# Edge sums by half tiles: one-hots side by side on PE, target rows spread on chip

## The chip, the cores and the metric

One core of one Trainium2 chip runs the whole model: a graph layer, a linear attention and a mixture of experts over 3125 nodes and 50,000 edges, in fp32. The metric is the device time of one execution in microseconds (us). The engines are named as in the profile: PE (TensorE, matrix products; PEld is its loading of stationary operands), DVE (VectorE), ACT (ScalarE), POOL (GpSimd, which also issues indirect DMAs) and SP (SyncE, which issues DMAs).

## The reference

Rows of 512 features are a scalar part of 128 and a vector part of 128x3. The change is in the edge part of the graph layer. Cut to what matters, with `x` the layer-normed rows:

```python
pd0, ip1 = p0[edge_dst], einsum('eum,eum->eu', p1[edge_dst], p1[edge_src]) / 3
w = ssp(edge_attr @ W_f1) @ W_f2 * (ssp(concat(pd0, pd0, ip1) @ W_s1) @ W_s2)
w1, w2, w3, w4 = split(w, 4)
x0e, x1e = split_irreps(x[edge_src])
out0 = w1 * x0e * sh0 + w4 * (einsum('eum,em->eu', x1e, sh1) / sqrt(3))
out1 = w2 * x0e * sh1 + w3 * x1e * sh0
out = segment_sum(concat(out0, out1), edge_dst, num_segments=3125)
```

`p0`, `p1` are linear maps of the rows, `ssp` is softplus less log 2, and `sh0`, `sh1` (one and three numbers) belong to the edge. Before it come layer norm, the node maps and a linear attention; after it an output map, a second layer norm, and eight experts of which each row takes two.

## The kernel before, in words

Three stages follow each other.

Stage 1 makes two tables in DRAM, `rows_d` (what an edge needs of its target: 32 hidden features and 384 of `p1`) and `rows_s` (what it needs of its source: 384 of `p1` and the 512 mapped features). Beside that it makes a record of 48 numbers for each edge (`records`, lines from 255: four `sh` numbers, both indices, the place of the target within its group in column 6, and 32 features of `ssp(edge_attr @ W_f1)`), and sorts the records by target. Targets are cut into 25 groups of 125. DVE counts the edges of each group (line 201), and `places(c)` (lines 229 to 252) finds the slot of each edge in chunk `c` of 14: a comparison with all groups, a running sum (line 239), a product and a reduction. POOL then writes 128 records at a time to their slots in `recs` (line 417, 391 times), between the node work. `recs` is cleared first (line 166). Each group's records begin at a new pair.

Stage 2 works through `recs`. Four tiles of 128 edges are a quad, two are a pair; 204 pairs are run. The order on PE, ACT, DVE and POOL is written out by hand in `run_pairs`, so that in step `s` different pairs are at different points: `fetch` (pair s+9) loads records and has POOL gather target rows `gd` (line 730) and source rows `gx` (line 734), one row per edge each; `products` (L746, DVE) multiplies the two `p1` parts; `turn` (L754, PE) sums and transposes the products, ACT copies them (L763); `hidden` (L770 to 780, PE) makes the hidden features of four tiles side by side in four column strips of the array; `softplus` (ACT) and `softplus2` (DVE) follow; `weigh` (L819, L823) makes the two factors of `w` on PE in four row strips, ACT copies one to SBUF and DVE multiplies by the other (L830). `dots` and `dots2` make the sum of vector features times `sh1` (L840 ACT, L848 and L850 DVE). `feats` (L878, L885, L889, L894) makes the features `ft`, with `sh1` applied by ACT. `which` (L860) makes a one-hot of the edge's target within the group, 128 wide, and `gather_up` (L902) multiplies one-hot by features, which sums the edges per target in PSUM. `keep_sums` (L911, DVE) adds a pair's sums to the group's rows of `acc`. Between pairs POOL issues copies of the expert weights into rows that can be gathered (`line_up`, L918, 32 of 1 MB).

Stage 3 maps the sums, writes `out`, normalizes, chooses experts, and runs 53 tiles of 128 rows through the experts' layers, with weights gathered by POOL.

Of the kernel before, what the change touches and what calls it, by code (L numbers as in the profile page):

```python
# [18 lines left out]
TG = 125  # L19
D = 512  # L20
# [11 lines left out]
NPR_MOST = 204  # L32
# [13 lines left out]
def gnn_mix_moe_kernel(ctx: ExitStack, tc: tile.TileContext, a: dict, out: bass.AP):  # L46
# [13 lines left out]
    NPR = (EDGES - NG) // (PR * P) + NG  # L60
    whole, rest_e = divmod(EDGES, P)
    TE = whole + (rest_e > 0)
    NQ = (NPR * PR + G - 1) // G
# [29 lines left out]
    pair_tile = const.tile([P, NPR], I32, name="pair_tile")  # L93


    rows_d = dram.tile([N, HID + 3 * MUL], F32, name="rows_d")
    rows_s = dram.tile([N, 3 * MUL + D], F32, name="rows_s")
    lined = dram.tile([T // CT, P, CT, REC], F32, name="lined")
    recs = dram.tile([NQ * G * P, REC], F32, name="recs")
# [20 lines left out]
    tok = counted(const, "tok", [[TG, NT]], [P, NT], channel=1)  # L120
# [8 lines left out]
    with ExitStack() as c1:  # L129
        srt = c1.enter_context(tc.tile_pool(name="srt", bufs=1))  # L130
        ints = c1.enter_context(tc.tile_pool(name="ints1", bufs=1))
        pair_no = counted(srt, "pair_no", [[1, NPR]], [P, NPR])
# [21 lines left out]
        for r in range(4):  # L154
# [6 lines left out]
        zw = NQ * G * REC // 10  # L161
        zero = tmp.tile([P, zw], F32, name="zero")
        nc.vector.memset(zero, 0.0)
        flat = recs.rearrange("s f -> (s f)")
        cleared = [
            nc.gpsimd.dma_start(
                flat[k * P * zw : (k + 1) * P * zw].rearrange("(p f) -> p f", p=P), zero
            )
            for k in range(10)
        ]  # L170

# [14 lines left out]
        in_tile_i = tmp.tile([P, T], I32, name="in_tile_i")  # L186
        nc.vector.tensor_scalar(in_tile_i, to_i, 4195.0, None, op0=ALU.mult)
        nc.vector.tensor_single_scalar(in_tile_i, in_tile_i, 19, op=ALU.arith_shift_right)
        in_tile = tmp.tile([P, T], F32, name="in_tile")
        nc.vector.tensor_copy(in_tile, in_tile_i)  # L190
        to_f = tmp.tile([P, T], F32, name="to_f")
        nc.vector.tensor_copy(to_f, to_i)
        local = tmp.tile([P, T], F32, name="local")
        nc.vector.scalar_tensor_tensor(local, in_tile, -float(TG), to_f, op0=ALU.mult, op1=ALU.add)

        NC = T // CT
        hot = tmp.tile([P, NT, CT + 1], F32, name="hot")
        sums = tmp.tile([P, NT], F32, name="sums")
        here = tmp.tile([P, T], F32, name="here")
        for b in range(NT):  # L200
            nc.vector.tensor_scalar(
                here, in_tile, float(b), 0.0, op0=ALU.is_equal, op1=ALU.add, accum_out=sums[:, b : b + 1]
            )
# [225 lines left out]
        for c in range(1, NC):  # L429
            records(c)  # L430
            for t in range((c - 1) * NT // (NC - 1), c * NT // (NC - 1)):
                place(8 * t + 42)
                place(8 * t + 50, layer_norm(t))
# [997 lines left out]
```

## Time and profile before

Times are of the device. The profiled execution is a separate one, slower than the runs without a profile.

| what | us |
|---|---|
| median of 3 runs (2772.86 to 2774.89) | 2774.01 |
| the profiled execution, own time | 2957.7 |
| its span, from the first to the last instruction | 2955.8 |
| stage 1: to the last node row (DMA of `rows_s`) | about 704 |
| stage 2: first gather to last sum | 721.9 to 2022.1 |
| first and last start of `gather_up`'s products | 774.4 and 2021.0 |
| PE busy in the span | 2533.0 (86%) |
| DVE busy | 1785.0 (60%) |
| ACT busy | 1393.6 (47%) |
| POOL busy | 1719.6 (58%) |
| mean granted clock of PE | 0.936 of full |

Three views of the profile are used. The windows view gives the busy time of each engine in a stretch of the span, with the number of instructions in brackets, then the clock granted to PE, the mean busy share of the 16 DMA engines, and what they moved. The timeline lists instructions in order of time: start, duration, engine, line of the kernel, operation, output and inputs by the program's names, shape, and how many were merged into the row; a bracket at the end tells idle time and what ended it. The view of groups gives, for all instructions of a line and shape, their busy time, the mean duration, and the idle time before them. A duration includes a fixed latency, so that the next instruction of an engine can start before it ends; the pitch, from start to start, is what an instruction costs in a full engine.

### The profile page before, as it was taken

What the parts mean: (1) busy time and instruction counts of PE and PEld (TensorE: products, weight loads), DVE (VectorE), ACT (ScalarE), POOL (GpSimd) and SP (SyncE); (2) the same over time, 40 slices, a digit from 0 to 9 for tenths busy, and PEclk for the clock granted to TensorE, in tenths of its full rate; (3) what the DMA queues carried; (4) which work ended last, traced back from release to release, by engine and by line L of the source; (5) the groups of instructions that cost most, each with busy time, mean ns of one, the idle gap of its engine ahead of it and who ended that gap; (6) DMA issues with size and microseconds to landing.
All of it is one profiled execution on the core that took longest, in us unless ns stands there. A gap on an engine that the chain in (4) does not pass through costs nothing. (4 is left out here: it accounts for less than half of the span.)

```text
span 2955.8 us, 44464 instructions
## 1 busy us (share of the span) xinstructions
PE 2533.0 (86%) x14742; PEld 1593.7 (54%) x14742; DVE 1785.0 (60%) x3666; ACT 1393.6 (47%) x3960; POOL 1719.6 (58%) x1723
## 2 busy tenths in 40 slices
PE   2466594885699999999999999997599999999997
PEld 2344242553344444444444444445488888888886
DVE  4755450223699999999999999998422222222221
ACT  1334241110588888877888888885211111111111
POOL 0766657664766666666666666641355555555552
PEclk9767796897799999999999999999799999999998
DMA  6435202554788888787888888855722623956361
GB/s 259 148 126 175 85 21 66 168 174 137 245 256 255 256 255 254 256 248 247 254 259 262 261 263 262 253 177 187 279 66 72 239 69 119 329 202 244 112 223 51
DMA packets 189190, 577.23 MB, mean 195 GB/s; under 512 B 54177, under 2 KB 78662, under 8 KB 176920
## 3 DMA queue, kind: packets, MB, share of 16 engines
q0 software_dynamic: 132912, 485.72, 51.1%
q1 hardware_dynamic: 49704, 82.29, 8.2%
q10 hardware_dynamic: 6336, 6.28, 0.7%
q8 instruction: 121, 1.98, 0.3%
q14 instruction: 117, 0.96, 0.1%
HBM read 624.55 MB, written 119.50 MB: 252 GB/s over the span
## 5 line engine op out<-in xcount | busy, mean ns | idle before, releaser
L902 PE MATMUL ps_s<-ft,one 128*128 128x512 f32 x1632 | 745.7, 600 | 19.4 <-issue 14.2
L730 POOL DMA_INDIRECT gd<-rows_d,rec x408 | 434.4, 1065 | 269.0 <-issue 87.2
L417 POOL DMA_INDIRECT recs<-again,at_i x391 | 400.8, 1025 | 231.6 <-issue 110.5
L902 PEld LDWEIGHTS ps_s<-ft,one 128*128 128x128 f32 x1632 | 294.1, 190 | 396.0 <-issue 318.7
L734 POOL DMA_INDIRECT gx<-rows_s,rec x408 | 400.9, 983 | 144.8 <-issue 102.4
L885 ACT ACTIVATE ft<-ft,rec 128x128 f32<-128x128 f32 x1224 | 380.2, 389 | 201.9 <-DVE ft L878 143.0
L1306 ACT ACTIVATE h<-ps_f,bias 128x128 f32<-128x128 f32 x318 | 110.7, 367 | 671.5 <-PE ps_f L1293 622.1
L1293 PE MATMUL ps_f<-h,we 128*128 128x128 f32 x3392 | 406.8, 278 | 16.7 <-ACT h L1306 15.1
L1293 PEld LDWEIGHTS ps_f<-h,we 128*128 128x128 f32 x3392 | 388.8, 192 | 30.7 <-ACT h L1306 25.0
L1308 DVE TENSOR_SCALAR h<-ps_f,bias 128x128 f32<-128x128 f32 x318 | 108.2, 350 | 481.6 <-PE ps_f L1293 456.9
L1220 POOL DMA_INDIRECT we<-w_rows,w_at x212 | 214.3, 1011 | 266.6 <-PE ps_y L1324 102.0
L830 DVE TENSOR_TENSOR wt<-wt,wb 128x1024 f32<-128x1024 f32 x204 | 247.6, 1214 | 29.9 <-PE ps_h L775 21.9
L840 ACT ACTIVATE dot<-gx,rec 128x128 f32<-128x128 f32 x816 | 261.4, 398 | 0.0
L819 PE MATMUL wa<-w_f,hT 32*128 32x512 f32 x816 | 240.2, 642 | 3.7 <-issue 2.6
L823 PE MATMUL wb<-w_s,hT 32*128 32x512 f32 x816 | 241.7, 644 | 0.0
L1293 PEld LDWEIGHTS ps_f<-xt,we 128*128 128x128 f32 x1696 | 200.1, 194 | 26.0 <-issue 24.9
L746 DVE TENSOR_TENSOR prod<-gd,gx 128x768 f32<-128x768 f32 x204 | 194.0, 951 | 31.0 <-DMA gx<-rows_s,rec 31.0
L1293 PE MATMUL ps_f<-xt,we 128*128 128x128 f32 x1696 | 200.5, 277 | 0.7 <-ACT xt L1241 0.7
L754 PEld LDWEIGHTS ps_ip<-ident,prod 128*128 128x128 f32 x1224 | 136.3, 144 | 118.7 <-issue 118.7
L889 DVE TENSOR_TENSOR ft<-gx,wt 128x768 f32<-128x768 f32 x204 | 197.6, 969 | 0.0
L1324 PE MATMUL ps_y<-we,h 128*128 128x512 f32 x424 | 196.1, 605 | 0.2
L754 PE MATMUL ps_ip<-ident,prod 128*128 128x128 f32 x1224 | 161.3, 283 | 40.7 <-issue 40.7
(306 smaller groups left out, 3599.2 us busy)
## 6 DMA issues: line engine op xcount, KB each, us to landing
w_rows<-in_Wh POOLq DMA_DIRECT2D x24, 1024.0 KB
rows_s<-r SPq DMA_DIRECT2D x24, 448.0 KB
recs<-zero POOLq DMA_DIRECT2D x10, 1056.0 KB
rec<-recs SPq DMA_DIRECT2D x102, 96.0 KB
lined<-rec SPq DMA_DIRECT2D x14, 672.0 KB
again<-lined POOLq DMA_DIRECT2D x14, 672.0 KB
w_rows<-in_Wo POOLq DMA_DIRECT2D x8, 1024.0 KB
gd<-rows_d,rec POOLq DMA_INDIRECT x408
```

The lines of the kernel that those rows point to most:

```text
L417: put = nc.gpsimd.indirect_dma_start(out=recs[:, :], out_offset=bass.IndirectOffsetOnAxis(ap=at_i[:m, t : t + 1], axis=0), in_=again[c][:m ...
L730: nc.gpsimd.indirect_dma_start(out=Q.gd[:, (i + 2) % G, :], out_offset=None, in_=rows_d[:, :], in_offset=bass.IndirectOffsetOnAxis(ap=reci ...
L734: Q.last = nc.gpsimd.indirect_dma_start(out=Q.gx[:, i, :], out_offset=None, in_=rows_s[:, :], in_offset=bass.IndirectOffsetOnAxis(ap=reci[ ...
L754: nc.tensor.matmul(ps[:, i, :], Q.prod[:, i, b * P : (b + 1) * P], ident, is_transpose=True, start=(b == 0), stop=(b == 2),)
L819: nc.tensor.matmul(wa[:, k, :], Q.hT[r, 0, :], w_f2[r, :], start=True, stop=True)
L823: nc.tensor.matmul(wb[:, k, :], Q.hT[r, 1, :], w_s2[r, :], start=True, stop=True)
L830: nc.vector.tensor_mul(R.wt, R.wt, wb)
L840: nc.scalar.activation(R.dot[:, c - 1, k, :], x[:, i, c * MUL : (c + 1) * MUL], AF.Copy, scale=Q.rec[:, i, c : c + 1])
L885: nc.scalar.activation(R.ft[:, k, D + c * MUL : D + (c + 1) * MUL], R.ft[:, k, 2 * D :], AF.Copy, scale=Q.rec[:, i, c : c + 1],)
L902: nc.tensor.matmul(R.ps, R.one[:, k, :], R.ft[:, k, m * D : (m + 1) * D], start=(k == 0 and m == 0), stop=(k == 1 and m == 1),)
L1220: nc.gpsimd.indirect_dma_start(out=dst, out_offset=None, in_=src, in_offset=bass.IndirectOffsetOnAxis(ap=at[:, j : j + 1], axis=0), bounds ...
L1293: nc.tensor.matmul(pss[f], ws[l][:, k, f * P : (f + 1) * P], h[:, k, :], start=(k == 0), stop=(k == 3))
```

## The change

Edges are sorted by 50 groups of targets, alternately 63 and 62, instead of 25 of 125. Two such groups make a half tile each; a pair now holds one tile of 128 edges from either half, and each half has room for 8 tiles (1024 edges) in a fixed place. Edges over that go to up to 12 overflow pairs behind the 200 fixed ones; for more there is a loop. Slots without an edge are no longer all cleared in DRAM: only the last quad of each group and the overflow pairs are, and records of slots without an edge are masked on chip (`clear`).

- The one-hot (`which`) is 64 wide and made per quad. ACT multiplies it by each of the four `sh` numbers (`scaled`), so `dots`, `dots2` and the `sh` steps of `weigh` and `feats` go. `feats` makes eight products of 128 features instead.
- `gather_up` puts the two halves in two column strips of 64 of the array, with four one-hots each: the first over 512 columns, the others over two runs of 128. All eight pairs of a group add up in one PSUM bank, which ACT copies to `acc` once (`kept`); only overflow pairs are still added by DVE.
- Target rows are no longer gathered per edge. `targets` loads the 64 rows of each half once per group on SP; `over` transposes the one-hots on PE, and `own_rows` multiplies them by the rows, in two row strips, which gives each edge its target's `p1` in PSUM. `products` reads it there; `hidden` takes the 32 hidden features by a product too.
- `weigh` alternates its two products, and ACT copies the first in one piece. `hidden2` copies the hidden features to SBUF before softplus.
- In stage 1, `places` counts over 50 groups and sends edges past 1024 to overflow slots; the expert weights are copied (`line_up`) from ACT's queue during stage 1.
- In the order written out, `keep_sums`, `softplus2` and `products` come first on DVE in a step, before `which`.
- `acc` holds 128 rows a tile, with two unused; stage 3 reads and writes each tile of `own` and `out` in two DMAs, and `xs` in one.

```diff
...
-NPR_MOST = 204
+NOV_MOST = 12
...
         cleared = [
-            nc.gpsimd.dma_start(
-                flat[k * P * zw : (k + 1) * P * zw].rearrange("(p f) -> p f", p=P), zero
-            )
-            for k in range(10)
+            nc.gpsimd.dma_start(by_quad[:, qs, :], zero[:, : G * REC].unsqueeze(1).to_broadcast([P, n, G * REC]))
+            for qs, n in (
+                (slice(per - 1, NFIX // PR, per), NG), (slice(NFIX // PR, (NFIX + NOV_MOST) // PR), NOV_MOST // PR),
+            )
         ]
...
-        for b in range(NT):
+        for b in range(NU):
...
+            nc.vector.tensor_copy(hot[:, :, 0], from_ if c == 0 else upto[:, :, CT])
...
+                hot[:, :, 1:], in_half[:, ts].unsqueeze(1).to_broadcast([P, NU, CT]),
+                lane[:, :NU].unsqueeze(2).to_broadcast([P, NU, CT]), op=ALU.is_equal,
...
+            nc.vector.tensor_mul(hot[:, :, 1:], upto[:, :, 1:], hot[:, :, 1:])
+            nc.vector.tensor_reduce(slot, hot[:, :, 1:].rearrange("p b i -> p i b"), AX.X, ALU.add)
             nc.vector.tensor_copy(slot_i, slot)
-            at = at_i[:, c * CT : (c + 1) * CT]
+            nc.vector.tensor_single_scalar(rank, slot_i, 65535, op=ALU.bitwise_and)
+            nc.vector.tensor_single_scalar(which, slot_i, 16, op=ALU.arith_shift_right)
+            nc.vector.scalar_tensor_tensor(moved, which, float(P), base_[:, ts], op0=ALU.mult, op1=ALU.subtract)
+            nc.vector.scalar_tensor_tensor(moved, rank, float(ROOM), moved, op0=ALU.is_ge, op1=ALU.mult)
+            nc.vector.scalar_tensor_tensor(moved, moved, far, base_[:, ts], op0=ALU.add, op1=ALU.add)
+            nc.vector.tensor_add(slot_i, moved, rank)
...
+        def line_up(behind):
+            if not mats:
+                return
+            e, l = mats.pop(0)
+            src = a["Wh"][e, l] if l < NL else a["Wo"][e]
+            with tc.issue_after(behind.ins):
+                nc.scalar.dma_start(
+                    w_rows[l][e * P : (e + 1) * P, :].rearrange("p (k f) -> p k f", k=4),
+                    src.rearrange("(k p) f -> p k f", p=P),
+                )
...
-        nc.vector.memset(acc, 0.0)
...
+        def clear(Q, real):
+            reci = Q.rec.bitcast(I32)[:, :, :USED]
+            nc.vector.tensor_tensor(
+                reci, reci, real.rearrange("p s k -> p (s k)").unsqueeze(2).to_broadcast([P, G, USED]),
+                op=ALU.bitwise_and,
+            )
...
+        def targets(b):
+            own = gat.tile([P, HID + 3 * MUL], F32, name="own", bufs=4)
+            for k in range(PR):
+                nc.sync.dma_start(own[k * HT : (k + 1) * HT, :], rows_d[bass.ds(b * TG + k * (HT - 1), HT), :])
+            return own
+        def which(Q):
+            Q.one = work.tile([P, G, HT], F32, name="one", bufs=6)
+            nc.vector.tensor_tensor(
+                Q.one, lane[:, :HT].unsqueeze(1).to_broadcast([P, G, HT]),
+                Q.rec[:, :, 6:7].to_broadcast([P, G, HT]), op=ALU.is_equal,
+            )
+        def over(Q):
+            ps = ps_a.tile([P, G, P], F32, name="ps_one", tag="turned")
+            for j in range(PR):
+                nc.tensor.transpose(
+                    ps[:, j, :], Q.one[:, PR * j : PR * (j + 1), :].rearrange("p k t -> p (k t)"), ident
+                )
+            Q.oneT = work.tile([P, PR, P], F32, name="oneT", bufs=4)
+            nc.scalar.copy(Q.oneT, ps[:, :PR, :])
+        def own_rows(R):
+            R.gd = ps_a.tile([P, PR, D], F32, name="gd")
+            for k in range(PR):
+                h = slice(k * HT, (k + 1) * HT)
+                nc.tensor.matmul(
+                    R.gd[:, k, : 3 * MUL], R.Q.oneT[h, R.j, :], R.own[h, HID:], start=True, stop=True,
+                    tile_position=(k * HT, 0),
+                )
+        def products(R):
+            Q, k = R.Q, R.j
             if k == 0:
                 Q.prod = work.tile([P, G, 3 * MUL], F32, name="prod")
             x = slice(2 * k, 2 * k + 2)
             d = slice(2 - 2 * k, 4 - 2 * k)
-            nc.vector.tensor_mul(Q.prod[:, d, :], Q.gd[:, d, HID:], Q.gx[:, x, : 3 * MUL])
-        def turn(q):
-            Q = quads[q]
-            ps = ps_a.tile([P, G, P], F32, name="ps_ip")
+            nc.vector.tensor_mul(Q.prod[:, d, :], R.gd[:, :, : 3 * MUL], Q.gx[:, x, : 3 * MUL])
...
+                R = Q.pairs[1 - i // PR]
+                h = slice(i % PR * HT, (i % PR + 1) * HT)
                 nc.tensor.matmul(
-                    Q.ps[i * HID : (i + 1) * HID, 1, :], Q.gd[:, i, :HID], ident,
-                    start=True, stop=False, tile_position=(0, i * HID),
+                    Q.ps[i * HID : (i + 1) * HID, 1, :], R.own[h, :HID], Q.oneT[h, R.j, :],
+                    start=True, stop=False, tile_position=(i % PR * HT, i * HID),
...
+        def hidden2(Q):
+            Q.hT = work.tile([P, 2, P], F32, name="hT", bufs=3)
+            nc.scalar.copy(Q.hT, Q.ps[:, :2, :])
...
+        def scaled(R, k):
+            if k == 0:
+                R.ones = work.tile([P, PR, 4, HT], F32, name="ones", bufs=3)
+            i = R.tiles[k]
+            for c in range(4):
+                nc.scalar.activation(
+                    R.ones[:, k, c, :], R.Q.one[:, i, :], AF.Copy, scale=R.Q.rec[:, i, c : c + 1]
+                )
...
+            for k, i in enumerate(R.tiles):
+                o = (i + 2) % G
+                r, q = slice(i * HID, (i + 1) * HID), slice(o * HID, (o + 1) * HID)
                 nc.tensor.matmul(wa[:, k, :], Q.hT[r, 0, :], w_f2[r, :], start=True, stop=True)
-            for k, i in enumerate(tiles):
-                i = (i + 2) % G
-                r = slice(i * HID, (i + 1) * HID)
-                nc.tensor.matmul(wb[:, k, :], Q.hT[r, 1, :], w_s2[r, :], start=True, stop=True)
+                nc.tensor.matmul(wb[:, k, :], Q.hT[q, 1, :], w_s2[q, :], start=True, stop=True)
             R.wt = work.tile([P, PR, D], F32, name="wt")
-            for k, i in enumerate(tiles):
-                nc.scalar.activation(
-                    R.wt[:, k, : 2 * MUL], wa[:, k, : 2 * MUL], AF.Copy, scale=Q.rec[:, i, 0:1]
-                )
-            nc.scalar.copy(R.wt[:, :, 2 * MUL :], wa[:, :, 2 * MUL :])
+            nc.scalar.copy(R.wt, wa)
             nc.vector.tensor_mul(R.wt, R.wt, wb)
...
+            R.ft = work.tile([P, PR, 8 * MUL], F32, name="ft")
             x = Q.gx[:, ts, 3 * MUL :]
+            w = R.wt.rearrange("p k (b c u) -> p k b c u", b=2, c=2)
             ends = bass.AP(
                 tensor=R.ft.tensor, offset=R.ft.offset,
+                ap=[list(R.ft.ap[0]), list(R.ft.ap[1]), [7 * MUL, 2], [1, MUL]],
             )
             nc.vector.tensor_mul(
+                ends, w[:, :, :, 0, :], x[:, :, :MUL].unsqueeze(2).to_broadcast([P, PR, 2, MUL]),
+            )
+            for k in range(PR):
+                nc.vector.tensor_mul(
+                    R.ft[:, k, MUL : 7 * MUL].rearrange("p (b c u) -> p b c u", b=2, c=3),
+                    w[:, k, :, 1, :].unsqueeze(2).to_broadcast([P, 2, 3, MUL]),
+                    x[:, k, MUL:].rearrange("p (c u) -> p c u", c=3).unsqueeze(1).to_broadcast([P, 2, 3, MUL]),
+                )
+        def gather_up(R, ps, first, last):
+            for m in range(4):
+                for k in range(PR):
+                    rows = slice(k * HT, (k + 1) * HT)
+                    if m == 0:
+                        to, what = ps[rows, :], R.ft[:, k, :D]
+                    else:
+                        o, f = ps[rows, :], R.ft[:, k, :]
+                        to = bass.AP(tensor=o.tensor, offset=o.offset, ap=[list(o.ap[0]), [m * MUL, 2], [1, MUL]])
+                        at = (3 + m) * MUL
+                        what = bass.AP(
+                            tensor=f.tensor, offset=f.offset + at, ap=[list(f.ap[0]), [7 * MUL - at, 2], [1, MUL]]
+                        )
+                    nc.tensor.matmul(
+                        to, R.ones[:, k, m, :], what, start=(first and m == 0), stop=(last and m == 3),
+                        tile_position=(0, k * HT),
                     )
...
+            def kept(at):
+                if not 0 <= at < n_pairs:
+                    return
+                R = pairs[at]
+                if at >= NFIX:
+                    keep_sums(tile_of(pair_tile[0:1, at - NFIX : at - NFIX + 1]), R.ps)
+                elif at % PER == PER - 1:
+                    nc.scalar.copy(acc[:, at // PER, :], R.ps)
+            for s in range(-LEAD - 5, n_pairs + 1):
+                for Q in due(s + LEAD + 5):
+                    q = quads.index(Q)
+                    loaded = load(Q, recs[q * G * P : (q + 1) * G * P, :])
+                    if q == 0:
+                        for put in placed:
+                            waits_for(loaded, put)
+                for R in pair(s + LEAD + 3):
+                    at = s + LEAD + 3
+                    if at >= NFIX:
+                        R.own = targets(
+                            nc.sync.value_load(pair_tile[0:1, at - NFIX : at - NFIX + 1], min_val=0, max_val=NG - 1)
+                        )
+                    elif at % PER == 0:
+                        R.own = targets(at // PER)
+                    else:
+                        R.own = pairs[at - 1].own
+                kept(s - 1)
+                for Q in due(s + 2):
+                    softplus2(Q)
+                for R in pair(s + 7):
+                    products(R)
+                for Q in due(s + LEAD + 1):
+                    q = quads.index(Q)
+                    clear(Q, real_slot[:, PR * q : PR * (q + 1), :])
+                    which(Q)
+                for Q in due(s + LEAD):
+                    over(Q)
+                for R in pair(s + 1):
+                    weigh(R)
+                for Q in due(s + 4):
+                    hidden(Q)
+                    hidden2(Q)
+                for Q in due(s + 3):
+                    softplus(Q, table)
+                for R in pair(s + LEAD):
+                    fetch(R.Q, R.j)
+                for R in pair(s + 2):
+                    scaled(R, 0)
+                for Q in due(s + 5):
+                    turn(Q)
+                    turn2(Q)
+                for R in pair(s + 2):
+                    scaled(R, 1)
+                for R in pair(s):
+                    if s >= NFIX or s % PER == 0:
+                        sums = ps_a.tile([P, D], F32, name="ps_s")
+                    R.ps = sums
+                    gather_up(
+                        R, R.ps, s >= NFIX or s % PER == 0, s >= NFIX or s % PER == PER - 1
                     )
+                for R in pair(s + 8):
+                    own_rows(R)
+                for R in pair(s + 1):
+                    feats(R)
...
+                    for k in range(2):
+                        i0 = t * TG + k * (HT - 1)
+                        m = min(HT, N - i0)
+                        nc.sync.dma_start(own[k * HT : k * HT + m], out[i0 : i0 + m, :])
...
-                    nc.gpsimd.dma_start(out[rows, :], base[:n, t, :])
+                    for k in range(2):
+                        i0 = t * TG + k * (HT - 1)
+                        m = HT - 1 - k
+                        nc.gpsimd.dma_start(out[i0 : i0 + m, :], base[k * HT : k * HT + m, t, :])
...
-                for i0, i1 in ((0, n - n % 16), (n - n % 16, n)):
-                    nc.sync.dma_start(xs[t * TG + i0 : t * TG + i1, :], xn[i0:i1])
+                nc.sync.dma_start(xs[t * P : (t + 1) * P, :], xn)
...
```

## The prediction

> **What bounds the kernel now.** I read the windows view first, to cut the profiled execution into stages, then the timeline of single engines inside the longest stage. One stretch of each stage:
>
> ```profile
> core 0: us, PE busy (x) PEld busy (x) DVE busy (x) ACT busy (x) POOL busy (x), PEclk, DMA share, GB/s
> 200.00:300.00 100.00, 68.74 (x279) 48.80 (x277) 62.39 (x220) 48.84 (x103) 69.67 (x68) 0.83 0.47 155
> ...
> 1700.00:1800.00 100.00, 100.00 (x576) 47.12 (x574) 98.71 (x173) 83.46 (x256) 68.70 (x70) 1.00 0.83 265
> ...
> 2400.00:2500.00 100.00, 98.39 (x712) 84.01 (x711) 24.93 (x65) 16.72 (x47) 53.18 (x54) 1.00 0.27 77
> ```
>
> Stage 1 (0 to 703 us: node features, edge records sorted to their places) has no full engine. Stage 2, the edge pairs, runs from the first gather (721.9 us) to the last sum (2022.1 us): 1300 us, of which 52 are filling before the first `gather_up` (774.4 us). Stage 3 (experts, to 2956 us) is PE alone. In stage 2 both PE and DVE look full, so a busy share does not name the bound. The timeline of PE over one quad (two pairs) does better:
>
> ```profile
> 1710.20 0.70 PE L819 MATMUL wa<-w_f,hT 32*128 32x512 f32 x2
> 1710.21 0.70 PE L823 MATMUL wb<-w_s,hT 32*128 32x512 f32 x2
> ...
> 1711.27 3.70 PE L902 MATMUL ps_s<-ft,one 128*128 128x512 f32 x8
> 1714.90 0.43 PE L770 MATMUL ps_h<-ident,rec 128*32 128x128 f32 x8
> ...
> 1715.36 0.40 PE L780 MATMUL ps_h<-ip,w_s1c 128*32 128x128 f32 x8
> ...
> 1717.30 1.53 PE L754 MATMUL ps_ip<-ident,prod 128*128 128x128 f32 x12
> 1718.66 3.60 PE L902 MATMUL ps_s<-ft,one 128*128 128x512 f32 x8
> 1722.19 0.70 PE L819 MATMUL wa<-w_f,hT 32*128 32x512 f32 x2
> ```
>
> From start to start: `weigh` 1.07 us, `gather_up` 3.63 or 3.53, `hidden` 0.79, `turn` 1.36; the other `weigh`, 1715.69 to 1717.30, takes 1.61, though its work is the same 1.07: PE waits there. The quad takes 11.99, PE needs 11.45 of it, 5.73 a pair. DVE in the same stretch:
>
> ```profile
> 1699.81 0.95 DVE L746 TENSOR_TENSOR prod<-gd,gx 128x768 f32<-128x768 f32 x1
> 1700.68 0.68 DVE L911 TENSOR_TENSOR acc<-acc,ps_s 128x512 f32 x1
> 1701.28 1.21 DVE L830 TENSOR_TENSOR wt<-wt,wb 128x1024 f32<-128x1024 f32 x1
> 1702.52 0.69 DVE L878 TENSOR_TENSOR ft<-wt,gx 128x512 f32<-128x512 f32 x1
> 1703.13 0.95 DVE L889 TENSOR_TENSOR ft<-gx,wt 128x768 f32<-128x768 f32 x1
> 1704.00 0.42 DVE L894 TENSOR_TENSOR ft<-wt,dot 128x256 f32<-128x256 f32 x1
> ```
>
> Its steps show no idle time: 0.87, 0.60, 1.24, 0.61, 0.87, 0.34 and on, and `prod` comes again after 11.94 us for two pairs. So DVE binds at 5.97 a pair, PE stands 0.24 behind, and the mean over the stage is 6.13 (1244 us over 203 steps). ACT is at 83%, the DMA engines at 83%: neither ends a wait that matters here.
>
> **What the Trainium skill says.** "TensorEngine Tiling (Array Packing)", Key Properties: tiles work side by side, each reading and writing its own partitions, and a change of tiling mode drains TensorE. "TensorE: Matmul & The Clock Gate", Part 3, measured 3.07 times for four row tiles and 2.38 for three column tiles. This trace agrees: a pass over 512 columns takes 0.427 us (pitch of the weight loads in `gather_up`), so eight passes of `weigh` one by one would be 3.42 and take 1.07; the 24 passes of `hidden`, in four column tiles, would be 2.57 and take 0.79. The drain shows as what lies over the ideal: 1.07 against 0.85, 3.63 against 3.42, 0.79 against 0.64; 0.1 to 0.2 us at each change. "VectorE: DVE Perf Modes", Mode 1x: one fp32 result a cycle with two tensor inputs, from PSUM too; the trace has 0.87 us for 768 elements and 1.24 for 1024 with a PSUM input.
>
> **The change, stage 2.** Pairs go from 204 to 212 (200 fixed and 12 for overflow; the inputs' counts need 10, so the loop for later ones is not entered).
>
> DVE, for each pair. Away: `acc` 0.60, the `dot` sum 0.45 and its two multiply-adds 0.54, `ft`<-`dot` 0.34, `one` 0.33. Kept: `prod` 0.87 (now with a PSUM operand), `wt` 1.24, `ft` of 512 0.61. The `ft` of 768 comes twice, 0.90 each. For each quad `softplus2` 0.20, `clear` (160 integers, between 0.2 and 0.33 by the 128 and 256 element rows: 0.24) and `which` 0.33, together 0.39 a pair. Sum 4.9 against 5.97.
>
> PE, for each pair. `gather_up` has a 64-column tile for each of the two edge tiles: one pass pair of 512 columns and three of 256, 2x0.427 + 6x0.213 = 2.13 if the two run side by side, 4.27 if not; the eight passes of four column tiles in `hidden` say they do. With 0.15 for the change of mode: 2.28. `own_rows` is new: two row tiles, two passes over 384 columns, 0.64 + 0.15 = 0.79. `weigh` stays 1.07. For each quad: `over`, two transposes, 0.21 + 0.1; `turn` 1.36; `hidden` 0.79 + 0.2, since its middle group is now in another mode than its neighbours. Sum 2.28 + 0.79 + 1.07 + (0.31 + 1.36 + 0.99)/2 = 5.5. The bounds: 5.2 when changes cost no more in all than now (0.5 a pair), 5.9 at 0.22 for each of the eleven changes of a quad.
>
> ACT, for each pair: ten 128-element steps (pitch 0.29) and three for `wt` go; eight of 64 elements come, 0.19 to 0.29 each, 0.26 taken, 2.1; the copy of 1024 about 0.9, the copies for `over`, `turn`, `hidden2` and softplus 2.1 a quad, `kept` 0.06. About 4.15, under PE: hidden by it. POOL issues two gathers instead of four, 2.5 us instead of 5.1 at a pitch of 1.26. The bytes of a pair fall from 1.34 MB to 0.92 of source rows, and the 0.21 MB of target rows are loaded once in eight pairs, on SP. So PE becomes the bound at 5.5 and every other engine has cover. The order holds: in a step PE does `weigh`, `hidden` or `turn`, `gather_up`, `own_rows`; the chain `weigh` - ACT copy - `wt` - `ft` is 1.0 + 1.2 + 2.4 = 4.6, and PE's own work between that `weigh` and its `gather_up` is about 6.8. The single `gd` buffer is read by `prod` about 3 us before `own_rows` fills it again; the shared `turned` bank is emptied by ACT one phase before its next use.
>
> Filling: it is paced by POOL, nine pairs of four gathers now (52 us), of two after: about 30. Overflow pairs have a target buffer each, four in all: `own_rows` of pairs 204, 206, 208 and 210 wait for a load that starts when `hidden` of the pair four back is done, with only `gather_up` between; about 2 us each, 8 in all. Stage 2 after: 30 + 211x5.5 + 3.5 + 8 = 1202. Gain 98.
>
> **Stage 1.** `places` works on 50 groups instead of 25: its scan (1.66), two products (0.88 each) and reduction (1.41) nearly double, +4.4, with six more small steps +0.7, for 14 chunks: 71. The counting loop goes from 25 to 50 of 0.64: +16. So 87 us more on DVE before 330 us, where windows of 100 us show it 52 to 62% busy; what is queued behind it is `fm` and `kf` of the layer norm, for which ACT and PE wait already. I take half on the path, 45; bounds 10 and 90. The clearing of `recs` shrinks from 10.5 to 3 MB; DVE waits 25 us for `sh` at the start behind it: -15. `pair_f`, ten steps of 1.3, is replaced by smaller ones: -5. The 32 copies of expert weights move from POOL in stage 2, where they were hidden, to ACT's queue in stage 1: 32 issues of 0.4 us, 32 MB more where the DMA share is 0.47; they may hold ACT when a queue slot is late: +5. Together +30. The memset of `acc` (10.7, while DVE waited for the records) costs nothing either way.
>
> **Stage 3.** Loads and stores of `own` and `out` are split in two (25 more issues on SP at 0.4, 25 more on POOL at 0.53, under a DVE pitch of 1.31 a tile: POOL gets about as long), `xs` writes are joined: 0, give or take 8.
>
> Sum: -98 + 30 = -68 us, of the profiled 2957.7, so 2890. The unprofiled median is 2774; the 184 us between them I put down to stage 1, where many waits have no named releaser ("remote") while stage 2 has 4 us of them. So I take the difference whole: 2774 - 68 = 2706.
>
> **Rivals.** (A) The forecast, PE at 5.5, 2706, own range 2660 to 2745: 0.5. (B) Mode changes overlap better and DVE binds at 4.95: stage 2 is 1086, 2590. For: single weight loads of 64 columns are shorter than of 128. Against: every phase of the trace pays. 0.15. (C) Slower: PE changes mode some eleven times a quad instead of five, and each costs 0.3 instead of 0.15[...]; that adds 0.8 a pair, 6.3, stage 2 is 1371 and the time 2875. It decides from 5.82 a pair on (41.5 + 211T = 1300 - 30). Against it stand the 0.1 to 0.2 measured now. 0.12. (D) DVE in stage 1 is all on the path, +90: 2766 with PE at 5.5. For: without the stalls of the profile stage 1 is shorter and DVE fuller. 0.15. (E) The column tiles of `gather_up` don't run side by side: 7.6 a pair, about 3150. Against: `hidden`. 0.03. The remaining 0.05 are mixtures near no change.
>
> **How the numbers follow.** 0.2% is about what a measurement here can tell from no change. Faster: A, B, most of D: 0.78. Slower: C, E and a tail of D with PE at 5.7: 0.17. Same: 0.05. The range 2610 to 2800 reaches from the low bound of PE (5.2, with stage 1 at 0) to D with PE at 5.65, and leaves B's far half, C and E outside.
>
> **What would show it.** Right: `ps_s` starts about 5.5 us apart with PE at 100% and DVE near 88%; `gather_up` about 2.3 from its start to the next phase, `own_rows` about 0.8; DMA share of stage 2 near 0.55; the first gather of stage 2 some 30 us later than 722. Wrong: a pitch at 4.9 (B), above 5.8 (C), PE waiting on DVE or ACT inside a step, or a first gather at 800 (D).

## The result and the profile after

The changed kernel takes 2765.95 us (median of 7 runs, 2765.16 to 2767.9), the kernel before 2774.01 (7 runs, 2772.51 to 2779.58): a ratio of 0.9969, 95% interval 0.9958 to 0.9981. The change gains 8 us, where 68 were forecast; the range (2610 to 2800) holds the time, the size of the gain is missed by far.

One thing has to be known to read what follows: the chips on which the runs were made differ. On those of the first kind the kernel before takes 2774 to 2778 us and its profiled execution as long as its others; on those of the second kind it takes 2957 and 3005 us, with idle times spread over the whole span. Each chip was met at one time only, so chip and moment can't be told apart; what makes the two kinds is open. By its time the profile of before that the prediction worked from (2957.7) is of the second kind, the median beside it of the first.

The windows view of the changed kernel (stretch in us, busy time of each engine with the number of instructions in brackets, clock granted to PE, DMA share, GB/s), one stretch of each stage:

```profile
core 0: us, PE busy (x) PEld busy (x) DVE busy (x) ACT busy (x) POOL busy (x), PEclk, DMA share, GB/s
200.00:300.00 100.00, 70.14 (x262) 45.27 (x263) 90.83 (x264) 50.43 (x107) 80.79 (x67) 0.88 0.76 264
...
1300.00:1400.00 100.00, 100.00 (x834) 46.86 (x834) 87.02 (x116) 70.92 (x212) 38.09 (x36) 1.00 0.55 175
...
2100.00:2200.00 100.00, 100.00 (x735) 86.91 (x734) 26.87 (x67) 18.78 (x47) 54.37 (x54) 1.00 0.58 194
```

In stage 2 PE is now full and DVE at 87%, as forecast; the DMA share fell from 0.83 to 0.55. In the stretch of stage 1 DVE is at 91%; before it was at 78% on a chip of the same kind (`before_third` below), 62% in the profile shown at the start. The timeline of PE over one quad (start, duration, line, operation):

```profile
1203.34 0.44 PE L849 MATMUL ps_one<-ident,one 128*128 128x128 f32 x2
1203.71 0.69 PE L956 MATMUL wa<-w_f,hT 32*128 32x512 f32 x1
...
1204.78 1.53 PE L879 MATMUL ps_ip<-ident,prod 128*128 128x128 f32 x12
1206.24 2.37 PE L998 MATMUL ps_s<-ft,ones 128*64 128x512 f32 x16
1208.54 0.92 PE L860 MATMUL gd<-own,oneT 64*128 64x384 f32 x4
1209.39 0.69 PE L956 MATMUL wa<-w_f,hT 32*128 32x512 f32 x1
...
1210.46 0.43 PE L893 MATMUL ps_h<-ident,rec 128*32 128x128 f32 x8
1210.82 0.42 PE L900 MATMUL ps_h<-oneT,own 64*32 64x128 f32 x8
1211.17 0.43 PE L905 MATMUL ps_h<-ip,w_s1c 128*32 128x128 f32 x8
1211.53 2.37 PE L998 MATMUL ps_s<-ft,ones 128*64 128x512 f32 x16
1213.83 0.92 PE L860 MATMUL gd<-own,oneT 64*128 64x384 f32 x4
1214.68 0.44 PE L849 MATMUL ps_one<-ident,one 128*128 128x128 f32 x2
```

The rows left out belong to the phases above them. From start to start: `over` 0.37 us, `weigh` 1.07, `turn` 1.46, `gather_up` 2.30, `own_rows` 0.85, `weigh` 1.07, `hidden` 1.07, `gather_up` 2.30, `own_rows` 0.85. This quad takes 11.34, a pair 5.67 (5.64 in the mean over the 211 steps), and PE never waits in it. DVE waits instead, in the same stretch 1.10 us for ACT's copy:

```profile
1205.95 1.22 DVE L960 TENSOR_TENSOR wt<-wt,wb 128x1024 f32<-128x1024 f32 x1 [1.10 <-ACT wt L959]
```

A profile of before that answers to its 2774 us came from a later run on a chip of the first kind (`before_third` below, 2777.57 us). The stages, from the starts of the first gather, the first `gather_up`, the last addition of a sum, and the span:

| kernel and chip | first gather | first `gather_up` | last sum | span | stage 1, 2, 3 |
|---|---|---|---|---|---|
| before, first kind (`before_third`) | 613.9 | 658.8 | 1871.4 | 2775.8 | 614, 1257.5, 904 |
| changed, first kind | 645.8 | 678.7 | 1873.1 | 2763.5 | 646, 1227.3, 890 |
| before, the profile shown | 721.9 | 774.4 | 2022.1 | 2955.8 | 722, 1300.2, 934 |
| before, second kind (`before_look`) | 708.9 | 758.6 | 2050.0 | 2992.1 | 709, 1341.1, 942 |
| changed, second kind (`after_look`) | 738.8 | 779.9 | 1975.0 | 2905.4 | 739, 1236.2, 930 |

On the chips of the result stage 1 grew by 32 us, stage 2 shrank by 30, stage 3 by 14: 12 us between the two profiles, 8 between the medians.

### The profile page after: what moved, and what is told of

It reads as the page before. It is cut to its first block, busy times and chain, and to the rows that moved or that the text cites. A ratio compares the mean times of both kernels' runs of the same rounds, so it can differ in the third digit from the quotient of the medians.

```text
span 2763.5 us, 47527 instructions
## 1 busy us (share of the span) xinstructions
PE 2458.9 (89%) x17776; PEld 1559.2 (56%) x17776; DVE 1701.4 (62%) x3084; ACT 1233.0 (45%) x3367; POOL 1356.8 (49%) x1319
## 5 line engine op out<-in xcount | busy, mean ns | idle before, releaser
L825 POOL DMA_INDIRECT gx<-rows_s,rec x424 | 464.1, 1095 | 717.1 <-DVE ft L978 603.8
L998 PE MATMUL ps_s<-ft,ones 128*64 128x256 f32 (+1 forms) x3392 | 505.2, 440 | 6.1 <-DVE acc L1006 6.1
L463 POOL DMA_INDIRECT recs<-again,at_i x391 | 424.4, 1085 | 164.9 <-issue 110.4
L944 ACT ACTIVATE ones<-one,rec 128x64 f32<-128x64 f32 x1696 | 437.6, 337 | 0.0
L978 DVE TENSOR_TENSOR ft<-wt,gx 128x768 f32<-128x768 f32 x424 | 385.5, 950 | 0.0
L998 PEld LDWEIGHTS ps_s<-ft,ones 128*64 128x64 f32 x3392 | 225.6, 137 | 230.7 <-issue 146.2
L960 DVE TENSOR_TENSOR wt<-wt,wb 128x1024 f32<-128x1024 f32 x212 | 259.0, 1222 | 138.3 <-ACT wt L959 114.1
L959 ACT COPY wt<-wa 128x1024 f32<-128x1024 f32 x212 | 214.8, 1013 | 201.1 <-PE wb L957 201.1
L872 DVE TENSOR_TENSOR prod<-gd,gx 128x768 f32<-128x768 f32 x212 | 201.0, 948 | 18.5 <-DMA rec<-recs 7.5
L860 PE MATMUL gd<-own,oneT 64*128 64x384 f32 x848 | 197.7, 540 | 10.1 <-DVE prod L872 8.2
L879 PEld LDWEIGHTS ps_ip<-ident,prod 128*128 128x128 f32 x1272 | 138.0, 142 | 80.8 <-ACT oneT L853 79.3
```

The costliest lines, as they stand in the source:

```text
L463: put = nc.gpsimd.indirect_dma_start(out=recs[:, :], out_offset=bass.IndirectOffsetOnAxis(ap=at_i[:m, t : t + 1], axis=0), in_=again[c][:m ...
L825: nc.gpsimd.indirect_dma_start(out=Q.gx[:, i, :], out_offset=None, in_=rows_s[:, :], in_offset=bass.IndirectOffsetOnAxis(ap=reci[:, i, 4:5 ...
L879: nc.tensor.matmul(ps[:, i, :], Q.prod[:, i, b * P : (b + 1) * P], ident, is_transpose=True, start=(b == 0), stop=(b == 2),)
L944: nc.scalar.activation(R.ones[:, k, c, :], R.Q.one[:, i, :], AF.Copy, scale=R.Q.rec[:, i, c : c + 1])
L959: nc.scalar.copy(R.wt, wa)
L960: nc.vector.tensor_mul(R.wt, R.wt, wb)
```

## The experiments

Theory at the outset: part of the gain was forecast from a stage 2 that the profile had stretched, and stage 1 grew by the doubled VectorE work (V). Rival: the copies of expert weights, moved into stage 1, hold up the scatters (C). The edits are shown shortened; words in place of code stand for lines left out.

**The kernel before, for another profile** (no edit), three times:

> The kernel before, unchanged, for a profile that isn't 184 us longer than its other runs. Theory 1 (part of the forecast gain was an artefact of that profile): first gather of stage 2 near 600 us instead of 722, the steps of stage 2 at 5.97 us throughout instead of 6.13 on average, stage 2 near 1265 instead of 1300, stage 3 near 890 instead of 934. Rival (all 184 us lay in stage 1, as I had taken it): first gather near 540, stage 2 at 1300, stage 3 at 934.

> The kernel before, unchanged, for a profile on the chip of this set of runs. On a chip where it takes 2774 us: scatters from 79 to 580 us, first gather of stage 2 at 600, steps at 5.97 us (stage 2 at 1265), stage 3 at 890. On one where it takes 2957 us it repeats the profile shown (first gather 715 to 722, stage 2 at 1284 to 1300).

> The kernel before, unchanged, once more for its profile. On a chip where it takes 2774 us: last scatter near 580 us, first gather near 600, steps at 5.97 us and stage 2 at 1265, stage 3 at 890. On one where it takes 2957 to 3005 us: as the two profiles before it.

The first two ran on chips of the second kind: 2958.67 us (20 runs, 2928.63 to 2985.46), and 2993.86 where the runs beside it have a median of 3004.89. The third ran on one of the first: 2777.57. Its steps are 5.97 us throughout (1211.9 from the first `gather_up` to its last, over 203), stage 2 is 1257.5 (1265 was expected), its first gather 613.9 (600), stage 3 904 (890). So the 180 us between the two spans lie in all three stages: 108 in stage 1, 43 in stage 2, 29 in stage 3. The same stretch of stage 2 in the windows of `before_third`:

```profile
1200.00:1300.00 100.00, 96.89 (x592) 45.83 (x592) 98.82 (x177) 82.94 (x259) 71.37 (x70) 1.00 0.85 266
```

and of `before_look`, with two rows from its view of waits between 800 and 2000 us (engine, what waited, for whom: us in total, times, longest):

```profile
1100.00:1200.00 100.00, 96.15 (x533) 45.20 (x532) 91.67 (x164) 76.92 (x238) 65.74 (x64) 0.97 0.76 237
```

```profile
DVE wt L830 <- PE ps_h L775: 31.1, 17, 2.2
DVE wt L830 <- ACT wt L829: 15.7, 6, 3.4
```

In `before_third` DVE has no row of this size: it is 98.8% busy in every stretch from 700 to 1800 us, and its waits between the first and last `gather_up` come to 3 us. In `before_look` it waits up to 3.4 us at a time; the two rows are 47 of the 79 us by which the time from the first `gather_up` to the last is longer there (1290.8 against 1211.9).

**The VectorE work of 50 groups alone**, in the kernel before:

```diff
-        for b in range(NT):
+        for b in range(2 * NT):          # 25 groups that no edge falls in
             nc.vector.tensor_scalar(here, in_tile, float(b), ..., accum_out=sums[:, b : b + 1])
-        hot, run, upto: [P, NT, CT + 1]; comparison, product, sum over NT groups
+        hot, run, upto: [P, 2 * NT, CT + 1]; comparison, product, sum over 2 * NT groups
```

This version also writes the product in place and keeps one `upto` instead of two, as the changed kernel does.

> The kernel before with 25 empty groups added to the counting loop and to places: the doubled VectorE work of the changed kernel's stage 1 alone, nothing else of the change. Theory V (this VectorE work is what lengthens stage 1): 35 to 50 us slower than before. Theory C (the copies of the expert weights, now in stage 1, lengthen it by slowing the scatters): 10 to 16 us slower, only the later first scatter. The forecast had half of 87, so 45.

2998.23 us against 2957.22, ratio 1.0138 (1.0076 to 1.0200): 41 us slower, as V says. Its first scatter comes at 103.1 us instead of 79.3. This is the price on a chip of the second kind.

**The copies of expert weights alone**, moved early in the kernel before and back to late in the changed one:

```diff
-                    if s >= lo and s % 6 == 0 and mats:      # in stage 2, POOL's queue
-                        line_up(*mats.pop(0))
+                line_up(normed)                              # in stage 1, ACT's queue
```

> The kernel before with the 32 copies of expert weights moved from POOL's queue in stage 2 to ACT's queue in stage 1, as the changed kernel has them, nothing else of the change. Theory C: 30 to 40 us slower, with scatters 1.5 us apart instead of 1.27 while the copies run. Theory V: within 5 us of before. Stage 2 may gain up to 15 us, 32 issues on POOL and 64 MB of traffic less, if the DMA share of 0.83 there mattered.

> The changed kernel with the 32 copies of expert weights put back to POOL's queue in stage 2, one in six steps as before. Theory C: 30 to 40 us faster than the changed kernel (about 2730), scatters back at 1.27 us apart between 100 and 300 us. Theory V: within 5 us of it (2766). Stage 2 should not change: POOL and the DMA engines have room there (0.39 and 0.55).

Early copies in the kernel before: 2951.2 against 2957.22, ratio 0.9983 (0.9959 to 1.0007), so the 30 to 40 us of C are excluded there. Late copies in the changed kernel: 0.9874 (0.9829 to 0.9919) of before on that chip, with the first gather at 749.1 us and stage 2 at 1238.9; with early copies, on another chip of the second kind, 738.8 and 1236.2: no sign of a gain, though across two chips. What the copies cost stage 1 alone is not settled: in the one profile with early copies the first gather comes at 736.3 us, against 714.0 in `before_again` on the same chip, but the first of these executions was 12 us above its median and the second 22 below. What tells V from C at the scatters themselves is the stretch from 100 to 200 us in the windows of POOL's scatters alone (busy time, number, clock, DMA share, GB/s), first of `before_again`, then of `before_fifty`, then of `before_early`, all on one chip:

```profile
100.00:200.00 100.00, 76.61 (x71) 0.77 0.53 168
```

```profile
100.00:200.00 100.00, 79.59 (x54) 0.77 0.46 144
```

```profile
100.00:200.00 100.00, 70.47 (x65) 0.74 0.60 199
```

A scatter takes 1.08 us in the kernel before, 1.47 with more VectorE work, 1.08 with more DMA traffic. Why does VectorE slow POOL? The timeline of the changed kernel, POOL first, DVE beneath:

```profile
186.82 0.96 POOL L463 DMA_INDIRECT recs<-again,at_i  x1 [0.31 <-issue]
188.08 3.06 POOL L463 DMA_INDIRECT recs<-again,at_i  x1 [0.30 <-issue]
191.45 1.67 POOL L463 DMA_INDIRECT recs<-again,at_i  x1 [0.30 <-issue]
193.42 0.95 POOL L463 DMA_INDIRECT recs<-again,at_i  x1 [0.30 <-issue]
```

```profile
187.22 3.16 DVE L276 TENSOR_TENSOR_SCAN upto<-run,hot 128x1450 f32<-128x1450 f32 x1
...
190.70 1.58 DVE L280 TENSOR_TENSOR hot<-upto,hot 128x1400 f32<-128x1400 f32 x1
...
192.33 2.59 DVE L281 TENSOR_REDUCE slot<-hot 128x28 f32<-128x1400 f32 x1
```

The scatter of 188.08 ends at 191.14, 0.76 us after the scan; that of 191.45 ends at 193.12, 0.84 after the product; that of 193.42, during the reduction, is not touched. Of the 152 scatters that start between 90 and 330 us, 45 take over 1.06 us, and all of these end 0.74 to 0.86 us after some VectorE operation; 32 of the 45 are matched to the comparison, scan and product of `places`, 8 to the sum of `so_far` and `b_add`, all of them reading two SBUF tensors. Since VectorE is nearly full, such a match can be chance (39 of the 107 short ones have it too). Sharper is what ran when a scatter started, with at least 0.35 us to go: all 33 that started in one of the three operations of `places` were long, none of the 33 that started in a reduction or in the statistics of the layer norm, which read one tensor. The Trainium skill has the mechanism ("SBUF — State Buffer", SBUF: two separate sides): VectorE and GpSimd share a port pair, an exclusive lock that a VectorE operation with two SBUF inputs holds to its end against a GpSimd operation that reads SBUF. This trace agrees, and shows that the issue of a scatter is held in this way. The three operations of `places` take 6.4 us a chunk; before they took 3.4.

The account of stage 1 closes with it. The groups of scatters up to 660 us, `before_third` and the changed kernel (busy us, mean ns, idle before by releaser):

```profile
L417 POOL DMA_INDIRECT recs<-again,at_i x391 | 402.6, 1030 | 142.3 <-issue 107.6 <-DVE b_row L394 22.3 <-DMA recs<-again,at_i 4.6
```

```profile
L463 POOL DMA_INDIRECT recs<-again,at_i x391 | 424.4, 1085 | 164.9 <-issue 110.4 <-DVE at_i L298 46.0 <-DMA recs<-again,at_i 3.7
```

Apart from the idle 0.3 us before each issue, the scatters follow each other with hardly a wait in both. The first starts at 79.3 and 90.6 us (11.3 later), the last at 608.6 and 640.5: the train is 529.3 and 549.9 us long (20.6 longer, 21.8 of it in the scatters' own durations). Together 31.9, all of stage 1's growth. A second chain grew as well: PE reaches the attention part (`ps_nm`) at 348.3 us instead of 312.6, 36 later, and its waits for `kf` (L382) rose from 6.8 to 29.5 us. But here no scatter waits for it, and the last row of `rows_s` is written at 560 us, 80 before the last scatter.

**The long operations of `places` cut into four**, in the changed kernel, and the kernel itself beside it:

```diff
+            parts = [slice(b * NU // 4, (b + 1) * NU // 4) for b in range(4)]
-            nc.vector.tensor_tensor_scan(upto, run, hot, ...)
+            for bs in parts:
+                nc.vector.tensor_tensor_scan(upto[:, bs], run[:, bs], hot[:, bs], ...)
             (comparison and product likewise)
```

> The changed kernel, unchanged, beside the kernel before on the same chip. Where before takes 2774 us: 2766. Where it takes 2957 us: if the early copies of weights cost nothing (as the run that moved them alone says), the same as with late copies, 2914; if they cost 30 to 40 us in the company of the doubled VectorE work, 2945 to 2955.

> The changed kernel with the three long VectorE operations of places (comparison, scan, product, 1.6, 3.16 and 1.6 us) each cut into four by groups; the work is the same, 126 instructions more on VectorE. Theory P (a scatter on POOL that starts while VectorE reads two SBUF tensors stands still until that operation is over; this makes scatters of 1.3 us in place of 0.96 and is what lengthens stage 1): scatters between 100 and 300 us fall from 1.25 to about 1.05 us, stage 1 ends 20 to 30 us earlier, the time falls by as much. Rival V1 (the chain of VectorE work itself is late, and the scatters wait for it): 126 more instructions at about 0.07 us make it 0 to 10 us slower, with scatters as long as before.

The changed kernel takes 2904.39 against 3004.89 there, a ratio of 0.966 (0.958 to 0.974): on this chip the change gains 100 us. The kernel with the operations cut takes 2910.15, no difference. The scatters did what theory P says: between 250 and 300 us, in `after_look` and then in `after_split`,

```profile
250.00:300.00 50.00, 40.28 (x31) 0.90 0.82 286
```

```profile
250.00:300.00 50.00, 34.23 (x32) 0.83 0.77 271
```

from 1.30 to 1.07 us each (1.22 and 1.07 over 100 to 350). But the end of stage 1 didn't move (first gather 738.8 and 742.6): on that chip the last row of `rows_s` (720.7 and 724.6 us) comes after the last scatter (713.7 and 717.8), so PE's work sets the end. That VectorE holds the scatters is shown, the 20 to 30 us are not.

**PE changes its tiling once less**, in the changed kernel:

```diff
         def hidden(Q):          # order of the three groups of eight passes
-            rec (128*32), own (64*32, start of ip), ip (128*32)
+            rec (128*32), ip (128*32, now the start), own (64*32)
```

> The changed kernel with the two groups of hidden that use 128-row tiles put side by side, the one with 64-row tiles last, so that PE changes its tiling once less in a quad; the work is the same. If each change of tiling costs 0.15 to 0.2 us on the path, as the phases of the trace say (0.36 us for a group whose passes alone would take 0.21), a quad of 11.33 us falls to 11.13 to 11.18 and the time by 16 to 21 us. Rival (the 0.15 belongs to each group, not to the change): no difference.

2894.35 us, a ratio to before of 0.9645 (0.9564 to 0.9725); the medians are 10 us apart, and the intervals of the two ratios overlap, so the times alone don't settle it. The traces are sharper: from the first `gather_up` to the last sum 1181.7 us instead of 1195.1, 0.13 a quad, less than the 0.15 to 0.2 expected. In its timeline `hidden` takes 0.92 from start to start (1209.18 to 1210.10), not 1.07; the second group, which no longer changes the tiling, starts 0.24 after the first instead of 0.36:

```profile
1209.18 0.42 PE L893 MATMUL ps_h<-ident,rec 128*32 128x128 f32 x8
1209.42 0.40 PE L898 MATMUL ps_h<-ip,w_s1c 128*32 128x128 f32 x8
1209.75 0.42 PE L905 MATMUL ps_h<-oneT,own 64*32 64x128 f32 x8
1210.10 2.16 PE L998 MATMUL ps_s<-ft,ones 128*64 128x512 f32 x14
```

**A version that beats both.** `after_both` has the last two edits; `after_count` also moves half of the counting loop to ACT, and `after_twelve` a quarter:

```diff
+        for k in range(NA + 1):        # NA = 25, then 12 groups
+            nc.scalar.activation(there, in_half, AF.Relu, bias=below[:, k : k + 1], accum_out=over_[:, k : k + 1])
+        sums[last NA] = over_[k] - 2 * over_[k + 1] + over_[k + 2]
```

> The changed kernel with the long operations of places cut into four and the groups of hidden put side by side, both from the runs before. Theory P: where scatters follow each other without waits (a chip where the changed kernel takes 2766 us) 20 to 35 us from stage 1 and 13 from stage 2, so 2720 to 2733. Where they wait for PE anyway (2904 us): only the 10 to 13 of stage 2, so about 2893.

> after_both with half of the counting loop (groups 25 to 49) taken from VectorE to ACT: sums of max(x - t, 0) for 26 thresholds, whose second differences are the counts. The first scatter comes 8 to 14 us earlier (at 70 to 76 us instead of 84). If the scatters set the end of stage 1, the time falls by that much against after_both; if the layer norm's chain does, by 0 to 5.

> after_count with 12 groups counted on ACT instead of 25, because there ACT became the late one (its sums waited between the softplus steps and were done at 59.5 us; VectorE then stood for 9 us). Expected: counts complete some 8 us earlier, first scatter at 76 to 80 us instead of 86.5; where before takes 2774 to 2778 us, stage 1 ends 5 to 10 us earlier and the time is 2730 to 2735 (ratio 0.984). If the scatters meet the wait for the layer norm's PE work again, as in after_both, they gain 0 to 4 us of it. On a chip with stalls: 0.96 to 0.97 of before.

All three ran on chips of the first kind. `after_both`: 2746.67, ratio 0.9891 (0.9869 to 0.9912). Stage 2 falls by 13.1 us to 1214.2, as the regrouping alone gave on the other kind of chip; stage 1 by 3.9, not by 20 to 35, because the faster scatters now run into the next wait:

```profile
POOL recs L468 <- PE ps_nm L652: 22.4, 2, 22.1
```

That is the wait that has POOL give way to PE in the attention part, which PE reaches at 369 us here and at 348 in the changed kernel; whether the cut operations delay PE by these 21 us, one profile of each doesn't show (in `after_split` it was 4). `after_count`: 2740.04, ratio 0.987 (0.985 to 0.9891). Its first scatter isn't earlier (86.5): ACT's sums stand between softplus steps and are done at 59.5 us only. The wait for PE is gone, since PE reaches that point earlier (358 us instead of 369), and the first gather is at 630.9: here the train of scatters is 539.1 us long, 10.8 shorter than in the changed kernel. `after_twelve`: 2735.11, ratio 0.9849 (0.9833 to 0.9866); the first scatter is at 71.7 us, 15 earlier, but POOL waits 18.5 us at the same place, and the first gather is at 629.0. It has the lowest ratio of those run, 1.5% below the kernel before, though its interval overlaps that of `after_count`.

## Why the prediction was wrong

By its steps:

- **"So I take the difference whole: 2774 - 68."** This failed. The prediction put the 184 us between profile and median down to stage 1, because waits without a named releaser came to only 4 us in stage 2, and so subtracted a new stage 2 from one of 1300 us. On a chip of the first kind stage 2 is 1257.5. That is 43 of the 68 us missing from its gain: 35 from steps of 6.13 us that are 5.97, 8 from the filling. The prediction had read the 5.97 as what DVE needs and the 6.13 as the mean, and didn't ask what the difference was. The difference stood in the same profile, in waits that do have a releaser:

```profile
DVE wt L830 <- PE ps_h L775: 21.9, 11, 2.2
```

With smaller rows DVE, the bound, waits 31 us between 800 and 2000 us, where `before_third` has 3 from the first `gather_up` to the last; by hundred microseconds it is 92.6 to 98.7% busy, and the stretch that the prediction shows is the fullest.

- **"Sum 2.28 + 0.79 + 1.07 + ... = 5.5."** The mechanism was right: PE is the bound, at 100%, the column tiles run side by side, DVE and ACT are at 4.9 and 4.0 us a pair (87 and 71% of 5.64) where 4.9 and 4.15 were forecast. The size was low: 5.67 by the timeline of a quad (`turn` 1.46 for 1.36, `hidden` 1.07 for 0.99, `over` 0.37 for 0.31, `own_rows` 0.85 for 0.79, `gather_up` 2.30 for 2.28). The mean of the 211 steps is 5.64, which makes 30 us; the filling took 33 us instead of 30, the 8 us for overflow pairs did not show, and the whole stage is 25 us longer than the 1202 forecast. The bound of 5.9 that the prediction gave for dearer changes of tiling covers it. `after_regroup` prices one change at 0.13 us; that a change drains the array is what the Trainium skill says too ("TensorEngine Tiling (Array Packing)", Key Properties).
- **Stage 1, +30.** Measured +32, and the nearness is luck. The prediction looked for the wait in the layer norm's `fm` and `kf`, half of it on the path. That chain did grow, by 36 us, but on a chip of the first kind it ends 80 us before the scatters, and they set the end: later by 11 and slowed by 21, a path that the prediction doesn't have. On the second kind its path fits: PE reaches the attention part at 407 us instead of 378, the last node row comes after the last scatter, and the first gather at 738.8 instead of 708.9. The 15 us for the smaller clearing and the 5 for the copies don't show as separate terms; the copies, early in the kernel before, cost between -12 and +2 us in all.
- **Stage 3, "0, give or take 8".** Measured -14: 6 up to the experts' first product, 2 in the experts, 6 after the last scatter is issued. In the first part ACT's 25 writes of normalized rows, joined, take 18 us instead of 36, and the split loads of `own` give back some 8. The last 6 stay open; no run was made for them.

So of the 60 us between forecast and result, 68 are stage 2's (43 on the side of before, 25 on that of after), 2 stage 1's, and stage 3 and the difference of medians and profiles give 10 back. The time of rival D, 2766, is what was measured, and D is still wrong: it had stage 1 at +90 and PE at 5.5. What PE did, 5.64, lies between the 5.5 of A and the 5.82 from which C counts.

On chips of the second kind, like the one of its profile, the forecast of 68 us is nearer, but not confirmed. On one the change gains 100 us (3004.89 to 2904.39) and stage 2 falls by 105 (1341.1 to 1236.2), where 98 were forecast; on the other the changed kernel with late copies gains 43 (2957.22 to 2914.25), and stage 2 falls by 47 (1285.6 in `before_again`, 1238.9). The changed kernel's stage 2 is nearly the same on both kinds of chip (1227, 1236, 1239), the one before isn't (1257 against 1286, 1300 and 1341). Why is not shown. That the stalls now fall on DVE (87%) and ACT (71%), which have room, is one reading; but PE, which has none, is hardly touched either: between 800 and 2000 us of `before_look` it stands 28 us with no named releaser, between 800 and 1900 us of `after_look` it waits 0.8 us in all. The changed kernel also issues half as many gathers, with a DMA share of 0.55 instead of 0.8, and no run separates the two.

## What to carry to other kernels

Compare the profiled execution with the runs before using its stages: when it is longer, ask each stage for its disturbance by setting its steady step against its mean and by adding up the waits of the engine that binds, named or not, and subtract new from undisturbed old. In this case the kernel with two engines near 97% lost 28 to 84 us of stage 2 on the disturbed chips and the one with PE alone full lost 9 to 12. And a VectorE operation with two SBUF operands can be paid twice when POOL issues indirect DMAs beside it. Cutting it into pieces shortens the hold, but brought 0 and 4 us of stage 1 here: look first what the issues wait for next.

## What was not expected

- A POOL scatter that starts during a two-operand VectorE operation on SBUF stands until that operation ends, and then takes all but 0.1 to 0.2 us of its usual 0.96; during a reduction of 2.6 us it isn't held. Four pieces of 0.9 us in place of one scan of 3.16 (and of 0.5 in place of the comparison and product of 1.6) bring the mean scatter from 1.22 to 1.07 us.
- The kernel before is 6.6 to 8% slower on some chips, the changed one 5% on the one where it was run as it is, though PE is granted nearly its full clock in stage 2 there (0.97 to 1.00); what causes the stalls is open.
